# Deformable attention near the grid: both image rows of a half tile in one product, and a fourth predicated copy

## The chip, the cores and the metric

The kernel runs on one core of a Trainium2 chip. The metric is device time in microseconds (us) of one whole execution. Six runs of the kernel before lie between 7702.01 and 7724.52 us, with a median of 7711.0 us.

## What is computed

The program is a network of four layers over x of shape (4, 64, 64, 128): four images of 64 by 64 positions with 128 channels. Only the first layer's convolution part, a deformable attention, is touched. Its reference, cut to what matters:

```python
# q, k, v: 1x1 projection of x, then a depthwise 3x3; four groups of 32 channels
for i in range(4):
    off = conv1x1(pconv(q_img, ...), w_off[i], b_off[i])      # 9 taps x (dy, dx) per position
    dil = 2 * i + 1                                           # 1, 3, 5, 7
    k_i = deform_sample(k[i], off, mask, dil, dil)            # bilinear, at tap + offset
    v_i = deform_sample(v[i], off, mask, dil, dil)
attn = softmax(einsum('bgnc,bgckn->bgnk', q * 32 ** -0.5, ks))   # 9 taps
out = einsum('bgnk,bgckn->bgnc', attn, vs) @ w_proj + b_proj
```

A bilinear sample whose offset is under one position in size is a weighted sum over the 3 by 3 neighbours of its tap. So a query's logit at a tap is a weighted sum of its products with the 9 keys around the tap. The kernel tests the offsets once and takes this local path (`deformable_near`) when they are all that small, as they are here.

## The kernel before, in words

`deformable_near` (from line 609) goes through 128 tiles. Tile T is a pair of image rows, 128 positions; tiles 32b to 32b+31 are image b. A tile has two halves of 32 columns (h), and each half two image rows (r). The partition of a position is 64h + 32r + 8m + x: m is a block of 8 columns, x the place in it. Four neighbouring tiles form a chunk c.

**Queries (lines 712 to 725).** `products` copies the queries of a tile with GpSimd into `qm`, which is zero but for the 8 queries of block m in the weights `qm[rows, j, m]`, 32 columns wide, j = 2h + r. Two such buffers alternate. The queries come from DRAM 16 image rows at a time (`rows_of_queries`, line 734, 512 KB each).

**Products (lines 739 to 757).** `product` multiplies queries with keys on TensorE in float32. For each block m of 8 columns, each j and each of the four dilations g (one per group of 32 channels, and so per group of 32 rows of the array), a matmul takes 32 by 32 weights from `qm` and streams 3 tap rows x 3 key rows x CW[g] key columns past them, CW = 12, 16, 20, 24: 108, 144, 180 or 216 columns. It writes 32 partitions of the PSUM tile S of its dilation and sums over m. That is 64 matmuls a tile. In the trace each stands as two weight loads (PEld) and two matmul records (PE).

**Copies (line 759).** `copy_products` moves the four S tiles to SBUF (`band`, with room for the four tiles of a chunk) on ScalarE, four copies a tile. There is one buffer of each S, so the next product waits for them; `band` has two.

**Attention (lines 765 to 793).** Once a chunk, on VectorE. A query at x in its block has its neighbours x columns further right, so three predicated copies (shift 4, 2 and 1, chosen by the bits of the partition's number, in `bit`) bring the rows of `band` into line, for each dilation: 12 copies a chunk (line 772). Twelve multiplications with the bilinear weights H (line 774), a sum and the maximum follow. ScalarE takes the exponential (line 797), `spread` turns the weights into a banded matrix A (line 804 onward), `write` sends A to DRAM (line 825), and `read_dense` reads it back as dense rows D (line 836).

**Values.** Fourteen tiles after its product (LAG), a tile's D is transposed on TensorE (`transpose`, line 867, 12 instructions, copied to SBUF by ScalarE on line 869) and multiplied with values (`weigh`, line 887, up to 48 matmuls). Every fourth tile there is a projection (line 910).

**Order.** The text of the loop gives the order on TensorE: transpose of T-14, product of T, now and then a projection, weigh of T-14. `block` and `behind` hold TensorE to that. Elsewhere a scheduler sets the order on each engine, from the order of the text and from what each instruction waits for. As built, on ScalarE the exponential of chunk c stands ahead of the copies of tile 4c+5, and on GpSimd the multiplications that make H of chunk c+3 stand behind the query copies of tile 4c+6. So VectorE's attention of a chunk has to be over before the second tile after it can leave PSUM.

Of the kernel before, what the change touches and what calls it, by code (L numbers as in the profile page):

```python
# [10 lines left out]
F32 = mybir.dt.float32  # L11
I32 = mybir.dt.int32
# [348 lines left out]
def window(ap, off, dims):  # L361

    return bass.AP(ap.tensor, ap.offset + off, [list(ap.ap[0])] + dims)
# [245 lines left out]
def deformable_near(k, dr, x, y, qd, kd, vd, od, masks, w_proj, b_proj):  # L609
# [15 lines left out]

    nc, tc = k.nc, k.tc
    DIL = (1, 3, 5, 7)  # L630
    W = [2 * d + 3 for d in DIL]
    WB = [5, 9, 15, 21]
    CW = [w + 7 for w in W]
    PP = [12 * (15 + w) for w in W]
    with ExitStack() as ctx:
        wp = ctx.enter_context(tc.tile_pool(name="dn_w", bufs=1))
        sm = ctx.enter_context(tc.tile_pool(name="dn_s", bufs=2))
        ps = ctx.enter_context(tc.tile_pool(name="dn_ps", bufs=1, space=PSUM))
# [5 lines left out]
        bit = wp.tile([128, 1, 3], I32, tag="bit", name="bit")  # L644
        nc.sync.dma_start(bit[:, 0, :], masks)
        kpad = wp.tile([128, 80, 80], F32, tag="kpad", name="kpad")
        nc.gpsimd.memset(kpad, 0.0)

        qms = [wp.tile([128, 4, 4, 32], F32, tag=f"qm{i}", name=f"qm{i}") for i in range(2)]
        for t in qms:  # L650
            nc.gpsimd.memset(t, 0.0)

# [18 lines left out]
        Hs, bands, outs, vblocks, logits, ofs, hat_of, queries = {}, {}, {}, {}, {}, {}, {}, {}  # L671
        accs, lefts, project, stores = {}, {}, [], []
# [6 lines left out]
        def block(do, *args):  # L679

            with behind():
                last[0] = do(*args)
# [31 lines left out]
        def products(T):  # L714
            i = T % 32
            c, t = divmod(T, 4)
            if t == 0:
                bands[c] = [sm.tile([128, 3, 4, 3, CW[g]], F32, tag=f"band{g}", name=f"band{g}") for g in range(4)]
            qm = qms[T % 2]
            q = queries[T // 8]  # L720
            for h in range(2):
                nc.gpsimd.tensor_copy(
                    window(qm, 256 * h, [[128, 2], [40, 4], [1, 8]]),
                    q[:, 2 * (i % 8) : 2 * (i % 8) + 2, 32 * h : 32 * h + 32].rearrange("p y (m x) -> p y m x", m=4),
                )

        def rows_of_keys(n):
# [4 lines left out]
            )  # L732

        def rows_of_queries(n):
            b, h = divmod(n, 4)
            queries[n] = sm.tile([128, 16, 64], F32, tag="q", name="q")
            nc.sync.dma_start(queries[n], qd[b].rearrange("p (y x) -> p y x", x=64)[:, 16 * h : 16 * h + 16, :])

        def product(T, half):
            if half == 0:  # L740
                accs[T] = [ps.tile([128, 9, CW[g]], F32, tag=f"S{g}", name=f"S{g}") for g in range(4)]
            i, qm, acc = T % 32, qms[T % 2], accs[T]
            for m in range(2 * half, 2 * half + 2):
                for j in range(4):
                    h, r = divmod(j, 2)
                    for g, d in enumerate(DIL):
                        rows = slice(32 * g, 32 * g + 32)
                        v = kpad[rows]
                        keys = bass.AP(
                            v.tensor, v.offset + (8 + 2 * i + r - d - 1) * 80 + 8 + 32 * h + 8 * m - d - 1,  # L750
                            [list(v.ap[0]), [80 * d, 3], [80, 3], [1, CW[g]]],
                        )
                        ins = nc.tensor.matmul(  # L753
                            acc[g][32 * j : 32 * j + 32].rearrange("p (a s) c -> p a s c", a=3),
                            qm[rows, j, m, :], keys, start=(m == 0), stop=(m == 3),
                        )
            return ins

# [6 lines left out]
        def attention(c):  # L765
            H, band = Hs[c], bands.pop(c)
            prod = sm.tile([128, 4, 36, 9], F32, tag="prod", name="prod", bufs=1)
            for g in range(4):
                flat = band[g].rearrange("p a t s c -> p (a t s) c")
                for i, s in enumerate((4, 2, 1)):  # L770
                    n = W[g] + s - 1
                    nc.vector.copy_predicated(flat[:, :, 0:n], bit[:, :, i : i + 1].to_broadcast([128, 36, n]), flat[:, :, s : s + n])  # L772
                for tx in range(3):
                    nc.vector.tensor_tensor(
                        window(prod, 324 * g + 9 * tx, [[27, 12], [3, 3], [1, 3]]),
                        window(band[g], DIL[g] * tx, [[3 * CW[g], 12], [CW[g], 3], [1, 3]]),
                        window(H, 324 * g + 9 * tx, [[27, 12], [3, 3], [1, 3]]), op=ALU.mult,
                    )
# [12 lines left out]
            nc.vector.tensor_tensor(lg, lg, each, op=ALU.subtract)  # L791
            logits[c] = lg, m, me, taps, wide, each
# [137 lines left out]
        rows_of_queries(0)  # L930
        offsets(0)
        products(0)
        for T in range(128 + LAG):
            with behind():
                step(T, -1, products)
                step(T, -2, offsets, 4)
                step(T, 0, hats, 4)
                step(T, 1, lambda c: hat_products(c, (0, 1)), 4)
                step(T, 2, lambda c: hat_products(c, (2, 3)), 4)
                step(T, 4, attention, 4)  # L940
                step(T, 7, spread, 4)
                step(T, 9, write, 4)
                step(T, LAG - 2, read_dense)
                step(T, LAG, values)
            V, P = 0 <= T - LAG, T < 128
            late = list(stores)
            if V:
                block(transpose, T - LAG)
            if P:
                block(product, T, 0)  # L950
                block(product, T, 1)
            if project:
                block(projection, *project.pop())
            if V:
                block(weigh, T - LAG)
            with behind():
                if late:
                    store()
                step(T, 0, copy_products)
                step(T, LAG, values_done)  # L960
                if T % 8 == 4 and T < 124:
                    rows_of_queries(T // 8 + 1)
                if T < 96:
# [9 lines left out]
def prep_conv0(w):  # L973
    g = lambda n: w["L0_conv_" + n]
    off = lambda a: a.reshape(4, 9, 2, -1).transpose(2, 0, 1, 3).reshape(72, -1)
    p = np.arange(128)
    grid = np.zeros((128, 2, 4, 3, 3), np.float32)
    for i in range(4):
        step = (np.arange(3) - 1) * (2 * i + 1)
        grid[:, 0, i] = (p // 64)[:, None, None] + step[None, :, None]  # L980
        grid[:, 1, i] = (p % 64)[:, None, None] + step[None, None, :]
    return {
        "c0_w_qkv": g("w_qkv"), "c0_b_qkv": g("b_qkv").reshape(3, 128).T, "c0_w_dw": g("w_dw").reshape(3, 128, 9).transpose(1, 0, 2),
        "c0_b_dw": g("b_dw").reshape(3, 128).T,
        "c0_pconv": np.concatenate([g("pconv_off_w"), g("pconv_mask_w")[None]]).reshape(5, 32, 32, 9).transpose(1, 0, 3, 2),
        "c0_w_offT": np.concatenate([off(g("w_off")), g("w_mask")]).T,
        "c0_b_off": np.concatenate([off(g("b_off"))[:, 0], g("b_mask")]),
        "c0_grid": grid.reshape(128, 72),
        "c0_masks": np.stack([p // 4 % 2, p // 2 % 2, p % 2], axis=1).astype(np.int32), "c0_w_proj": g("w_proj"), "c0_b_proj": g("b_proj"),
    }  # L990


# [1614 lines left out]
```

## Time and profile before

| what | us |
|---|---|
| median of six runs | 7711.0 |
| the profiled execution, whole | 7687.94 |
| its span, first to last instruction | 7686.1 |
| `deformable_near`: first product to last weigh | 678 to 1823 |
| tiles 0 to 13, products alone | 678 to 770 |
| tiles 14 to 127, products and values (114 steps) | 770 to 1750 |
| last 14 tiles, values alone | 1750 to 1823 |

| 770 to 1750 us | busy us of 980 | a step (of 8.60 us) |
|---|---|---|
| TensorE matmuls | 735.96 | 6.46 |
| VectorE | 492.79 | 4.32 |
| ScalarE | 321.44 | 2.82 |
| GpSimd | 398.29 | 3.49 |
| DMA, mean share of 16 engines | 0.71 | 6.1 |

How to read it: all steps of the middle stretch do the same work, so 980 us / 114 gives one step, and the busy time of an engine can be divided the same way. The profiled execution is 23 us shorter than the median of the runs. DMA is given as a mean share over 16 engines, 0.71 x 8.60 = 6.1 us of all sixteen a step. In the names, `PEld` is TensorE's weight load, `PE` its matmul; SP issues most of the DMAs, ScalarE the others.

### The profile page before, as it was taken

The page shows a single profiled execution, that of the slowest core. Times are in us where ns is not written, and L with a number is a line of the kernel's source. Part 1 is how long each engine was busy: PE and PEld are TensorE (multiplying, and loading weights), DVE is VectorE, ACT ScalarE, POOL GpSimd, SP SyncE. Part 2 cuts the span into 40 slices and gives each one's busy share as a digit, 9 for nine tenths or more (in the row PEclk, how much of TensorE's full clock was granted, in tenths as well). Part 3 has the DMA queues.
Part 4 walks back from the last instruction along what each step waited for, and adds up shares of the span by engine and source line. Part 5 has one row for each costly group of instructions (what it writes and reads, how often), then busy time and mean ns, then how long its engine had stood idle before and what let it go on. Part 6 is the DMA issues. An engine that isn't in the chain of part 4 may idle for free. (4 is left out here: it accounts for less than half of the span.)

```text
span 7686.1 us, 173919 instructions
## 1 busy us (share of the span) xinstructions
PE 6524.1 (85%) x71983; PEld 3530.2 (46%) x71983; DVE 4663.4 (61%) x11050; ACT 2679.8 (35%) x6141; POOL 1753.1 (23%) x1634
## 2 busy tenths in 40 slices
PE   7996777775688868979989999798798997997989
PEld 3343656563456544345555555445225224242244
DVE  2214555454277654858855666675785885867877
ACT  3331333333234323611145656565104013031056
POOL 0003443430001100035532222154012012120135
PEclk9997888987788889989988999798897997998989
DMA  4436677775400022031000000001111111111101
GB/s 120 100 89 183 191 212 204 205 202 167 143 4 1 2 60 48 4 119 27 23 16 9 10 9 8 9 1 30 38 25 41 34 31 43 25 35 38 25 23 31
DMA packets 676539, 496.62 MB, mean 65 GB/s; under 512 B 302070, under 2 KB 593848, under 8 KB 671896
## 3 DMA queue, kind: packets, MB, share of 16 engines
q1 hardware_dynamic: 478606, 354.58, 17.0%
q10 hardware_dynamic: 197130, 130.77, 6.2%
q8 instruction: 572, 9.37, 0.5%
q14 instruction: 231, 1.89, 0.1%
HBM read 335.28 MB, written 149.75 MB: 63 GB/s over the span
## 5 line engine op out<-in xcount | busy, mean ns | idle before, releaser
L2476 DVE TENSOR_TENSOR t<-S,q 128x1536 f32<-128x1536 f32 (+3 forms) x608 | 1157.0, 1948 | 121.2 <-PE S L2464 115.9
L2464 PE MATMUL S<-R,L 32*128 32x512 f32 x4096 | 734.5, 651 | 89.9 <-DMA R<-wd 78.5
L2492 PE MATMUL acc<-t,sum 128*32 128x512 f32 x4096 | 639.6, 608 | 0.0
L772 DVE COPY_PREDICATED band<-bit,band 128x288 f32<-128x288 int32 (+11 forms) x384 | 244.1, 748 | 468.5 <-ACT band L763 450.7
L753 PE MATMUL S<-kpad,qm 32*32 32x216 f32 (+3 forms) x16384 | 398.0, 344 | 138.8 <-issue 78.4
L2178 PE MATMUL pe<-ew,yT 128*128 128x512 f32 x1024 | 479.3, 602 | 26.3 <-DVE xs L2184 23.3
L1777 PE MATMUL acc<-w,attT 128*64 128x264 f32 x4096 | 485.7, 390 | 11.9 <-DVE w L1773 11.9
L2464 PEld LDWEIGHTS S<-R,L 32*128 32x128 f32 x4096 | 200.3, 186 | 611.0 <-issue 279.9
L2498 ACT COPY agg<-acc 128x512 f32<-128x512 f32 x32 | 18.7, 585 | 1191.8 <-DMA L<-pd 681.4
L1770 POOL TENSOR_TENSOR w<-xtl,ei 128x528 f32<-128x528 f32 x256 | 331.8, 1317 | 314.1 <-ACT ei L1769 204.4
L2184 DVE SCALAR_TENSOR_TENSOR xs<-pe,gate,xs 128x128 f32<-128x128 f32 x1024 | 332.8, 345 | 96.2 <-PE pe L2178 79.6
L753 PEld LDWEIGHTS S<-kpad,qm 32*32 32x32 f32 x16384 | 275.9, 110 | 230.5 <-issue 133.3
L1773 DVE TENSOR_TENSOR w<-xtl,pe 128x1056 f32<-128x1056 f32 x256 | 320.2, 1251 | 101.4 <-ACT ei L1769 88.8
L1777 PEld LDWEIGHTS acc<-w,attT 128*64 128x64 f32 x4096 | 283.7, 137 | 198.6 <-DVE w L1774 38.3
L2187 ACT ACTIVATE sc<-pe,gate 128x128 f32<-128x128 f32 x1024 | 290.3, 374 | 200.8 <-PE pe L2178 193.7
L2507 POOL TENSOR_TENSOR o<-o,bf 128x512 f32<-128x512 f32 x32 | 40.6, 1269 | 1228.1 <-ACT o L2506 1228.1
L514 PE MATMUL dw<-pad,diag 32*32 32x512 f32 x6912 | 308.0, 617 | 11.2 <-ACT dwo L522 5.8
L887 PE MATMUL out<-dt,vb 128*32 128x32 f32 x12000 | 177.7, 208 | 149.4 <-issue 141.2
L2492 PEld LDWEIGHTS acc<-t,sum 128*32 128x32 f32 x4096 | 92.7, 108 | 458.6 <-issue 436.2
L763 ACT COPY band<-S 128x108 f32<-128x108 f32 (+3 forms) x512 | 113.7, 308 | 514.1 <-PE S L753 175.6
L2178 PEld LDWEIGHTS pe<-ew,yT 128*128 128x128 f32 x1024 | 185.4, 193 | 232.7 <-issue 151.0
L869 ACT COPY dt<-pt 128x512 f32<-128x512 f32 x384 | 209.4, 598 | 208.2 <-PE pt L867 201.6
(519 smaller groups left out, 12911.1 us busy)
## 6 DMA issues: line engine op xcount, KB each, us to landing
vb<-vd SPq DMA_DIRECT2D x272, 256.0 KB
D<-dd ACTq DMA_DIRECT2D x128, 192.0 KB
D<-dd SPq DMA_DIRECT2D x128, 168.0 KB
D<-dd ACTq DMA_DIRECT2D x128, 144.0 KB
w<-in_e_weight_dram ACTq DMA_DIRECT2D x16, 1024.0 KB
w<-in_e_weight_dram SPq DMA_DIRECT2D x16, 1024.0 KB
wd<-s SPq DMA_DIRECT2D x32, 512.0 KB
D<-dd SPq DMA_DIRECT2D x128, 120.0 KB
```

Source lines behind the costliest of these rows:

```text
L514: nc.tensor.matmul(acc[g][32 * c : 32 * c + 32], diag[r, j, tap, :], pads[j][r, y0 : y0 + 8, tx : tx + 64], start=(tap == 0), stop=(tap == 8),
L753: ins = nc.tensor.matmul(acc[g][32 * j : 32 * j + 32].rearrange("p (a s) c -> p a s c", a=3), qm[rows, j, m, :], keys, start=(m == 0), sto ...
L772: nc.vector.copy_predicated(flat[:, :, 0:n], bit[:, :, i : i + 1].to_broadcast([128, 36, n]), flat[:, :, s : s + n])
L1770: nc.gpsimd.tensor_tensor(w2[:, 2:4], xt[:, 2:4, 0:2], window(ei, 0, [[0, 2], [0, 2], [1, 132]]), op=ALU.mult)
L1773: nc.vector.tensor_tensor(w1, xt[:, :, 1:3], window(pe, 0, [[0, 4], [0, 2], [1, 132]]), op=ALU.mult)
L1777: nc.tensor.matmul(acc[b // 2][64 * (b % 2) : 64 * (b % 2) + 64], attT[:, b // 2, hp, 64 * (b % 2) : 64 * (b % 2) + 64], src[:, b].rearran ...
L2178: nc.tensor.matmul(pe[h].rearrange("p e c -> p (e c)"), yT[:, 128 * t : 128 * t + 128], ew[:, 4 * h : 4 * h + 4, :].rearrange("p e c -> p ...
L2184: nc.vector.scalar_tensor_tensor(xt, pe[0][:, e, :], gate[:, t, e : e + 1], xt, op0=ALU.mult, op1=ALU.add)
L2187: nc.scalar.activation(sc[:, e, j, :], pe[1][:, e, :], AF.Copy, scale=gate[:, t, 4 + e : 5 + e])
L2464: nc.tensor.matmul(S[:, j, :], Ls[n % 2][r, ag, :], Rs[n % 2][r, ag].rearrange("p x y -> p (x y)"), start=True, stop=True)
L2476: nc.vector.tensor_tensor(t[:, j0:j1].rearrange("p u (x y) -> p u x y", x=8), S[:, j0:j1].rearrange("p u (x y) -> p u x y", x=8), qf[:, q0 ...
L2492: nc.tensor.matmul(acc[0][32 * h : 32 * h + 32, :], sum4, t[:, j, :], start=(u < 4), stop=(u >= 60))
```

## The change

One matmul now serves both image rows of a half tile. Its weights are 64 columns wide (both rows' 8 queries of block m, at 32r + 8m), it streams 4 key rows instead of 3 (144, 192, 240 or 288 columns), and it writes 64 partitions of S. So there are 32 matmuls a tile instead of 64. Row r = 0 needs key rows 0 to 2 and row r = 1 key rows 1 to 3. S and `band` hold 4 key rows, and a fourth predicated copy for each dilation moves key rows 1 to 3 down by one on the partitions with r = 1: 12 runs of 3 CW elements. The other three copies work on the same sizes as before, in rows that now lie 4 CW apart. The queries come 8 image rows at a time (32 loads of 256 KB instead of 16 of 512 KB).

```diff
-        qms = [wp.tile([128, 4, 4, 32], F32, tag=f"qm{i}", name=f"qm{i}") for i in range(2)]
+        qms = [wp.tile([128, 2, 4, 64], F32, tag=f"qm{i}", name=f"qm{i}") for i in range(2)]
...
-                    window(qm, 256 * h, [[128, 2], [40, 4], [1, 8]]),
+                    window(qm, 256 * h, [[32, 2], [72, 4], [1, 8]]),
...
-            for m in range(2 * half, 2 * half + 2):
-                for j in range(4):
-                    h, r = divmod(j, 2)
+            for m in range(4):
+                for h in range(2):
                     for g, d in enumerate(DIL):
...
-                            v.tensor, v.offset + (8 + 2 * i + r - d - 1) * 80 + 8 + 32 * h + 8 * m - d - 1,
-                            [list(v.ap[0]), [80 * d, 3], [80, 3], [1, CW[g]]],
+                            v.tensor, v.offset + (8 + 2 * i - d - 1) * 80 + 8 + 32 * h + 8 * m - d - 1,
+                            [list(v.ap[0]), [80 * d, 3], [80, 4], [1, CW[g]]],
...
-                            acc[g][32 * j : 32 * j + 32].rearrange("p (a s) c -> p a s c", a=3),
-                            qm[rows, j, m, :], keys, start=(m == 0), stop=(m == 3),
+                            acc[g][64 * h : 64 * h + 64].rearrange("p (a s) c -> p a s c", a=3),
+                            qm[rows, h, m, :], keys, start=(m == 0), stop=(m == 3),
...
-                flat = band[g].rearrange("p a t s c -> p (a t s) c")
+                rows = lambda off, dims: window(band[g], off, [[4 * CW[g], 12]] + dims)
+                n = 3 * CW[g]
+                nc.vector.copy_predicated(rows(0, [[1, n]]), bit[:, 0, :, 3:4].to_broadcast([128, 12, n]), rows(CW[g], [[1, n]]))
                 for i, s in enumerate((4, 2, 1)):
                     n = W[g] + s - 1
-                    nc.vector.copy_predicated(flat[:, :, 0:n], bit[:, :, i : i + 1].to_broadcast([128, 36, n]), flat[:, :, s : s + n])
+                    nc.vector.copy_predicated(
+                        rows(0, [[CW[g], 3], [1, n]]), bit[:, :, :, i : i + 1].to_broadcast([128, 12, 3, n]), rows(s, [[CW[g], 3], [1, n]])
+                    )
...
-                if T % 8 == 4 and T < 124:
-                    rows_of_queries(T // 8 + 1)
+                if T % 4 == 1 and T < 124:
+                    rows_of_queries(T // 4 + 1)
```

More of the change, by code (lines that the diff above doesn't have):

```diff
@@ L643, in deformable_near @@
         nc.sync.dma_start(bpj[:, 0, :], b_proj.partition_broadcast(128))
-        bit = wp.tile([128, 1, 3], I32, tag="bit", name="bit")
-        nc.sync.dma_start(bit[:, 0, :], masks)
+        bit = wp.tile([128, 1, 1, 4], I32, tag="bit", name="bit")
+        nc.sync.dma_start(bit[:, 0, 0, :], masks)
         kpad = wp.tile([128, 80, 80], F32, tag="kpad", name="kpad")
         nc.gpsimd.memset(kpad, 0.0)
-        qms = [wp.tile([128, 4, 4, 32], F32, tag=f"qm{i}", name=f"qm{i}") for i in range(2)]
+        qms = [wp.tile([128, 2, 4, 64], F32, tag=f"qm{i}", name=f"qm{i}") for i in range(2)]
         for t in qms:
@@ L717, in products @@
             if t == 0:
-                bands[c] = [sm.tile([128, 3, 4, 3, CW[g]], F32, tag=f"band{g}", name=f"band{g}") for g in range(4)]
+                bands[c] = [sm.tile([128, 3, 4, 4, CW[g]], F32, tag=f"band{g}", name=f"band{g}") for g in range(4)]
             qm = qms[T % 2]
-            q = queries[T // 8]
+            q = queries[T // 4]
             for h in range(2):
                 nc.gpsimd.tensor_copy(
-                    window(qm, 256 * h, [[128, 2], [40, 4], [1, 8]]),
-                    q[:, 2 * (i % 8) : 2 * (i % 8) + 2, 32 * h : 32 * h + 32].rearrange("p y (m x) -> p y m x", m=4),
+                    window(qm, 256 * h, [[32, 2], [72, 4], [1, 8]]),
+                    q[:, 2 * (i % 4) : 2 * (i % 4) + 2, 32 * h : 32 * h + 32].rearrange("p y (m x) -> p y m x", m=4),
                 )
@@ L734, in rows_of_queries, with product @@
         def rows_of_queries(n):
[L735 to L741, printed above, removed]
+            b, h = divmod(n, 8)
+            queries[n] = sm.tile([128, 8, 64], F32, tag="q", name="q")
+            nc.sync.dma_start(queries[n], qd[b].rearrange("p (y x) -> p y x", x=64)[:, 8 * h : 8 * h + 8, :])
+        def product(T):
+            accs[T] = [ps.tile([128, 12, CW[g]], F32, tag=f"S{g}", name=f"S{g}") for g in range(4)]
             i, qm, acc = T % 32, qms[T % 2], accs[T]
-            for m in range(2 * half, 2 * half + 2):
-                for j in range(4):
-                    h, r = divmod(j, 2)
+            for m in range(4):
+                for h in range(2):
                     for g, d in enumerate(DIL):
@@ L775, in attention @@
                         window(prod, 324 * g + 9 * tx, [[27, 12], [3, 3], [1, 3]]),
-                        window(band[g], DIL[g] * tx, [[3 * CW[g], 12], [CW[g], 3], [1, 3]]),
+                        window(band[g], DIL[g] * tx, [[4 * CW[g], 12], [CW[g], 3], [1, 3]]),
                         window(H, 324 * g + 9 * tx, [[27, 12], [3, 3], [1, 3]]), op=ALU.mult,
@@ L949, in deformable_near @@
             if P:
-                block(product, T, 0)
-                block(product, T, 1)
+                block(product, T)
             if project:
@@ L988, in prep_conv0 @@
         "c0_grid": grid.reshape(128, 72),
-        "c0_masks": np.stack([p // 4 % 2, p // 2 % 2, p % 2], axis=1).astype(np.int32), "c0_w_proj": g("w_proj"), "c0_b_proj": g("b_proj"),
+        "c0_masks": np.stack([p // 4 % 2, p // 2 % 2, p % 2, p // 32 % 2], axis=1).astype(np.int32), "c0_w_proj": g("w_proj"), "c0_b_proj": g("b_proj"),
     }
```

## The prediction

> **What bounds the kernel now.** I read the windows first, then who waits, the DMA queues, the timeline and the groups. The window of the 114 steps that do both products and values (columns: length, busy time and instructions by engine, granted clock, DMA share, GB/s):
>
> ```profile
> 770.00:1750.00 980.00, 735.96 (x26677) 595.21 (x26664) 492.79 (x1503) 321.44 (x878) 398.29 (x544) 0.88 0.71 202
> ```
>
> TensorE (first pair) is busy 75% of it, and nothing else is busier. The waits of TensorE in the same stretch say what fills the other 244 us:
>
> ```profile
> PE out L887 <- issue: 134.8, 78, 4.3
> PE S L753 <- issue: 76.0, 66, 3.5
> PE pt L867 <- issue: 11.8, 6, 3.2
> PE S L753 <- POOL qm L722: 6.3, 8, 1.3
> PE pr L910 <- issue: 5.8, 2, 3.6
> PE S L753 <- ACT band L763: 3.9, 3, 3.1
> ```
>
> Four rows end in "issue", 228 us together: no semaphore is waited for, the engine has nothing to issue. The DMA queues of the stretch and TensorE's timeline tell why:
>
> ```profile
> q8 instruction: 209, 3.42, 1.5%
> ```
>
> ```profile
> 1205.84 0.40 PE L887 MATMUL out<-dt,vb 128*32 128x32 f32 x24 [0.89 <-issue]
> 1206.17 1.64 PE L867 MATMUL pt<-ident,D 128*128 128x128 f32 x12
> 1207.74 1.83 PE L753 MATMUL S<-kpad,qm 32*32 32x108 f32 x91
> 1211.42 1.08 PE L753 MATMUL S<-kpad,qm 32*32 32x144 f32 x37 [1.85 <-issue]
> ```
>
> Queue q8 brought 209 packets of 16 KB; 26677 + 26664 matmuls and weight loads over 209 packets are 255 each. Between the two stalls stand 24 + 12 + 91 matmuls, with their weight loads some 255 again. So TensorE runs dry at packet ends. In the trace, packets start 4.70 us apart in the mean (a twentieth under 3.5, a twentieth over 6.8); 186 of 209 are followed, 1.4 us after they land, by the end of a stall. **TensorE is bound by the arrival of its instructions:** busy 735.96 / 209 = 3.52 us a packet, waiting 1.1.
>
> **The change part by part, for one step of 8.60 us.**
>
> *Fewer instructions.* 53341 / 114 = 468 matmuls and weight loads a step. A product has 64 matmuls x 4 records = 256; it gets 128. So 340 remain, 1.33 packets for 1.83. At 4.70 us a packet that is 6.25 us.
>
> *The streams.* The groups by form:
>
> ```profile
> L753 PE MATMUL S<-kpad,qm 32*32 32x216 f32 x4096 | 384.6, 397 | 19.1 <-issue 18.7
> ...
> L753 PE MATMUL S<-kpad,qm 32*32 32x108 f32 x4096 | 332.2, 288 | 79.9 <-POOL qm L722 39.2 <-issue 21.0 <-ACT band L763 19.1
> ...
> L2367 PE MATMUL po<-pn 32*64 32x64 f32 x2048 | 87.2, 337 | 0.0
> ```
>
> 397 - 288 ns over 108 columns is 1.01 ns a column, and 179 ns that don't depend on it. One position of the array is visited by 4 blocks x 2 records in turn: 8 x 216 x 1.01 = 1.75 us for dilation 7, + 0.18 = 1.9 us, where a product is busy 2.99 us (341.1 us of the stretch / 114). With 288 columns the same chain is 2.3 + 0.18 = 2.5 us, the lower end; with the old excess of 1.06 us kept, 3.6, the upper. Half as many weights should shrink the excess: I take 2.9, no gain. The form 32*64 stands on line 2367: 243.2 us busy for 6144 records, 40 ns each at 337 ns long, so such tiles overlap. TensorE is then busy 6.46 - 2.99 + 2.9 = 6.4 us a step, 4.8 a packet.
>
> *The two together.* A packet now takes as long to work off (4.8) as the next one to come (4.7, spread about 1.05): the wait does not vanish, about half the packets are late. With a spread of 0.7 for the work, the mean lateness is 0.4 x sqrt(1.05² + 0.7²) = 0.5 us; 1.33 x 0.5 = 0.7, and 6.4 + 0.7 = **7.1 us a step**, 1.5 less. 114 x 1.5 = 171 us.
>
> The Trainium skill, "Runtime: NRT & Kernel Launch", section "Instruction fetch mechanics", agrees on blocks of 256 instructions but calls the cost of crossing one mostly hidden. By it the instruction count is worth nothing and the change brings about 0.1 us a step, 10 in all; the rows above speak against it. "TensorEngine Tiling (Array Packing)", section "Available Configurations", has 16 tiles of 32x32 but 8 of 32x64: by that count alone a product would take 4/3, 4.0 us, and a step 8.0 or so. The busy time of 2.99 against a chain of 1.9 says that the tiles were not what bound it.
>
> *The fourth predicated copy,* 4 more a chunk. An old one of a dilation takes 475 to 1000 ns and hardly depends on its shift: its mean is near 1.1 ns x 36 x CW. The new ones have as many elements, 12 x 3 CW, 2592 together: by these rows 475 + 650 + 820 + 990 = 2.9 us. By the reduction on line 781 (1503 ns for 1296 elements) 3.0; by the dearest row (482 ns for 180) 2.7 x 2592 = 6.9, the upper end. I take 3.0, the shape being nearest to whole rows; the old ones overlap (244.1 us busy for 384 of 748 ns: 0.85), so 2.6. VectorE goes from 4.32 to 5.0 us a step: hidden in its idle time:
>
> ```profile
> DVE band L772 <- ACT band L763: 415.2, 28, 19.9
> ```
>
> But it lengthens the path copies of tile 4c+3, attention, exponential, copies of 4c+5. Attention now lasts 11.9 us (1193.4 to 1205.3), then 14.5. Behind the exponential on ScalarE wait the copies of 4c+5, and for them the product of 4c+6. From their end to the copies of 4c+7 are two steps, less transpose and weigh, already done by then (230.0 + 155.7 us / 113 = 3.4): 14.2 - 3.4 = 10.8. The circle is 14.5 - 0.6 (overlap) + 0.35 + 0.9 + 10.8 = 26 us for four steps, under 28.4. Covered, by 2.4 us; without that cover each us more costs 0.25 a step.
>
> *Copies out of PSUM:* 248 to 372 ns for 108 to 216 elements, 1.15 ns each; 216 elements more a tile, 0.25 us, beside 3.4 us of transpose and weigh. Nothing.
>
> *Queries:* GpSimd copies as many elements; nothing. 16 more SP issues of 0.45 us, 7 us over 980 of a queue that issues 5.6 us a step (now of 7.1): nothing. They stand between dense reads four tiles ahead of use; late ones would hold GpSimd and then the product.
>
> *DMA:* the same bytes in less time, 6.1 / 7.1 = 86% busy. Instruction packets share the engines with them; in the trace, with 16 or more packets in flight the next instruction packet starts 2.5 us after a stall's end, with under 4 in flight 1.4. I leave the mean at 4.7; 5.2 would cost 0.4 us a step.
>
> *First 14 tiles:* in their window TensorE waits 33.0 us for qm from GpSimd, 15.1 for copies of S, and only 2.4 on issue; nothing gained, three attentions of 2.6 us more, at most 8: I take 6. *Last 14:* no products; the last attention has 50 us until its tiles come: nothing.
>
> Sum: -171 + 6 = -165 us. The profiled execution of 7688 becomes 7523; it ran 23 us under the median of 7711, from which I forecast **7546**.
>
> **The rivals.**
>
> *Fed, but not faster (a step of 7.5 to 8.0).* TensorE's chain takes the place of the wait: a product at its upper 3.6 makes 7.1 busy and about 7.7 a step, -97 us. Or VectorE's circle: attention at its upper end of 18.8 makes 30.3 / 4 = 7.6, -110 us. For: both lie within 0.6 us of the bound. Against: the 1.06 us excess looks like issue, and the copies' rows are even.
>
> *Better (6.5).* Refills stay at 4.7, the product falls to 2.5, the clock (0.88) rises because TensorE pauses less: -235 us. Against: DMA would be 94% busy.
>
> *It does nothing.* Refills slow down as DMA grows denser, a packet coming every 6.4 us: 1.33 x 6.4 = 8.5, no change. Against: even with 16 in flight the delay grew by 1.1 us only.
>
> *Slower.* The fourth copy in VectorE's circle: it decides once four steps exceed 34.4 us, that is attention above 22.6 + 0.3 us, the new copies over 11 us a chunk. At twice the dearest row, 5.4 ns x 2592 = 14 us, attention is 25.9, the circle 37.3, 9.3 us a step: +0.7 x 114 = +80 us. For: no row shows a copy of 12 long runs whose source overlaps its target. Against: no f32 row costs a third of that.
>
> **How the numbers follow.** Forecast (6.8 to 7.4 a step) 0.52; fed but not faster 0.19; better 0.17; nothing 0.05; slower 0.07. The predicted time is that of the first. From -240 to -60 us holds 8 in 10: 7470 to 7650. Within 0.2% (15 us, about what measurement can tell from no change) 0.05; faster 0.88; slower 0.07.
>
> **What would show it.** Right: some 152 packets on q8 in the middle stretch instead of 209, about 4.9 us apart; "issue" under 130 us instead of 228; a product busy near 2.9 us; the new copies 0.5 to 1 us each; ScalarE's wait for line 791 small. Wrong: packets 6 us apart; TensorE waiting for S copies behind the exponential; a product over 3.6 us.

## The result

The changed kernel takes 7691.8 us (median of 37 runs), the kernel before 7705.6 us (77 runs): the ratio is 0.9984, 95% interval 0.9978 to 0.9990, some 12 us less. The forecast was 7546. The two profiled executions lie closer still, 7686.57 against 7687.94.

By stages of the profiled executions (before, after): tiles 0 to 13 take 88.1 and 93.2 us, a step of tiles 14 to 127 takes 8.67 and 8.54 us (by the starts of the products), the last 14 tiles take 76.8 and 79.7. So the middle gained 113 x 0.13 = 15 us, where 171 had been forecast, and the ends lost 8.

The window of the middle stretch, in the columns of the one shown of before:

```profile
770.00:1750.00 980.00, 740.88 (x19763) 619.20 (x19752) 666.64 (x1654) 330.33 (x886) 371.22 (x541) 0.84 0.71 205
```

TensorE did its work with 74% of the instructions, and its busy time, like its idle time, is what it was: 239 us idle for 244. The DMA share did not move either, 0.71 and 205 GB/s for 202. What TensorE waits for is another matter (waited for, total us, times, longest):

```profile
PE S L750 <- ACT band L760: 103.1, 48, 6.1
PE S L750 <- POOL qm L721: 73.6, 14, 9.4
PE out L888 <- issue: 44.9, 34, 4.7
PE S L750 <- issue: 4.7, 3, 3.4
PE pt L868 <- issue: 4.7, 4, 2.4
```

The queue of instruction packets:

```profile
q8 instruction: 155, 2.54, 1.1%
```

155 packets for 209, and 54 us of "issue" for 228: the wait that the change was priced by is gone. In its place stand 103 us for ScalarE's copies of S, which free the PSUM that the next product writes, and 74 us for GpSimd's copies of queries. Both had been 10 us together. 174 us went and 167 came.

So why are those copies late? ScalarE's waits after the change:

```profile
ACT band L760 <- DMA D<-dd: 138.4, 27, 7.2
ACT lg L798 <- DMA D<-dd: 82.3, 10, 11.2
ACT band L760 <- DMA dd<-A: 50.1, 13, 5.2
ACT lg L798 <- DMA kpad<-kd: 49.7, 6, 9.6
```

and the same engine before:

```profile
ACT dt L869 <- PE pt L867: 172.2, 145, 5.5
ACT band L763 <- DMA D<-dd: 155.9, 35, 7.9
...
ACT band L763 <- DMA dd<-A: 22.0, 5, 5.0
```

A copy of S into `band` reads neither D nor dd. The releaser belongs to what stands ahead of the copy on ScalarE: half of the dense reads (line 837) are issued there. In the program as built, all transfers that SyncE and ScalarE issue share eight semaphores in turn (in the trace the numbers 100 and 102 to 108), and each waits at its issue for the landing of the one eight before it. That is a limit of the program and not of the chip: at most eight transfers in flight. There are 45 of them in four steps, and each lands 4.2 us after its issue has ended, 4.8 us after it began. One place shows how it reaches TensorE. SyncE's queue, ScalarE's and TensorE, in three views of the timeline of after (start, length, engine, instruction, how often in a row; in brackets the idle time before it):

```profile
1262.85 5.68 SPq L826 DMA_DIRECT2D dd<-A  x7
1268.63 1.27 SPq L837 DMA_DIRECT2D D<-dd  x2
```

```profile
1263.14 1.61 ACT L870 COPY dt<-pt 128x512 f32<-128x512 f32 x3
1269.20 1.22 ACTq L837 DMA_DIRECT2D D<-dd  x2
1270.46 1.07 ACT L760 COPY band<-S 128x144 f32<-128x144 f32 x4 [5.71 <-DMA D<-dd]
```

```profile
1263.51 2.20 PE L750 MATMUL S<-kpad,qm 32*64 32x144 f32 x64
1265.64 1.04 PE L888 MATMUL out<-dt,vb 128*32 128x32 f32 x96
1266.61 1.63 PE L868 MATMUL pt<-ident,D 128*128 128x128 f32 x12
1270.88 4.56 PE L750 MATMUL S<-kpad,qm 32*64 32x144 f32 x64 [2.64 <-ACT band L760]
```

The product ends at 1265.7 and ScalarE is idle, but it stands at its next dense read until 1269.20: the transfer eight before is one of SyncE's writes, which landed at 1269.18. The copies start 4.8 us late, TensorE 2.64 us late, and its next product runs at half the speed, 4.56 us for 2.20. Over tiles 20 to 123, such waits at ScalarE's issues (idle time over 0.15 us ahead of an issue whose own semaphore came last) add up to 223 of 907 us before and 379 of 893 us after; the expectations below have 205 and 358, by another count. For 347 of the 379 us the transfer eight before was in flight; for the rest SyncE had not issued it yet or was issuing it.

The same can be followed for all of TensorE's waits on ScalarE in the stretch. For 93 of the 103 us, ScalarE's last idle time ahead of the copy ended with the landing of a DMA, for 5 us with VectorE. In 50 of the 93 us it is the exponential that stood at the transfers, ahead of the copies.

GpSimd in the same stretch of after:

```profile
POOL xg L905 <- DMA xg<-in_x_dram: 350.8, 20, 24.8
```

The sum of tokens and bias stands ahead of the copies of queries, and waits for a load that comes late in the same line of transfers. With two smaller rows such waits are 456 us; before, they were 208.5 ("issue") and 44.8 us. For 71 of the 74 us that TensorE waits for queries, GpSimd's last idle time was of this kind.

### The profile page after: what moved, and what is told of

It is laid out like the page before. It is cut to its first block, busy times and chain, and to the rows that moved or that the text cites. A ratio compares the mean times of both kernels' runs of the same rounds, so it can differ in the third digit from the quotient of the medians.

```text
span 7683.6 us, 157708 instructions
## 1 busy us (share of the span) xinstructions
PE 6518.5 (85%) x63791; PEld 3548.7 (46%) x63791; DVE 4828.8 (63%) x11178; ACT 2687.1 (35%) x6141; POOL 1727.9 (22%) x1634
## 5 line engine op out<-in xcount | busy, mean ns | idle before, releaser
L750 PE MATMUL S<-kpad,qm 32*64 32x288 f32 (+3 forms) x8192 | 412.5, 425 | 236.9 <-POOL qm L721 119.7
L750 PEld LDWEIGHTS S<-kpad,qm 32*64 32x64 f32 x8192 | 306.5, 157 | 293.9 <-issue 138.4
L760 ACT COPY band<-S 128x144 f32<-128x144 f32 (+3 forms) x512 | 136.0, 351 | 458.6 <-DMA D<-dd 146.2
L768 DVE COPY_PREDICATED band<-bit,band 128x432 f32<-128x432 int32 (+3 forms) x128 | 108.5, 902 | 256.8 <-ACT band L760 216.6
L868 PE MATMUL pt<-ident,D 128*128 128x128 f32 x1536 | 236.7, 309 | 17.5 <-DMA D<-dd 8.2
```

The source lines that it names most:

```text
L750: ins = nc.tensor.matmul(acc[g][64 * h : 64 * h + 64].rearrange("p (a s) c -> p a s c", a=3), qm[rows, h, m, :], keys, start=(m == 0), sto ...
```

## The experiments

Times are ratios to the kernel before, run beside each kernel on the same chip; the change itself is 0.9984. Each expectation spells out the theories that it weighs.

**Without the fourth copy.** The changed kernel less the one new line on VectorE (so the lower image row's products stay out of line in the result).

```diff
-                nc.vector.copy_predicated(rows(0, [[1, n]]), bit[:, 0, :, 3:4].to_broadcast([128, 12, n]), rows(CW[g], [[1, n]]))
```

> The changed kernel without its four predicated copies a chunk that move key rows 1 to 3 down (left out: that move, so the products of every second image row stay out of line). Theory A, the circle of VectorE and ScalarE: in the changed kernel copies of tile 4c+3, attention (15.0 us), exponential (2.9 us later, behind two dense-read issues on ScalarE), copies of tile 4c+5, product of 4c+6 set the four steps of 34.5 us. Without the copies attention lasts 12.0 us and the scheduler puts the exponential ahead of the reads: four steps of 29 to 32 us, 70 to 150 us less than the kernel after. Theory B, transfers: ScalarE and GpSimd are held by landings of dense reads and of the token loads, and VectorE's length does not matter: within 15 us of the kernel after.

Measured: 0.9964 (0.9948 to 0.9981), some 15 us under the changed kernel, give or take 14. Attention is back at 12 us and VectorE at 495 us, and TensorE still waits for the same engines, most of all for ScalarE's copies of the transposed D:

```profile
PE out L887 <- ACT dt L869: 77.6, 32, 4.7
PE S L750 <- ACT band L760: 61.7, 30, 6.6
PE pt L867 <- ACT o L912: 35.1, 14, 5.7
PE S L750 <- POOL qm L721: 32.0, 24, 2.5
```

The fourth copy takes about a tenth of the missing gain of 153 us, at most a fifth. The edit also moved the exponential: here it stands ahead of the next dense reads on ScalarE, in the changed kernel behind two of them. So the 15 us are for both together, and VectorE's circle as the main cause falls.

**The kernel before, with copies of the same size added** (each onto itself, so the result stays).

```diff
+                wide = band[g].rearrange("p a t s c -> p (a t) (s c)")
+                nc.vector.copy_predicated(wide, bit[:, :, 3:4].to_broadcast([128, 12, n]), wide)
...
```

> The kernel before with four more predicated copies a chunk of the size of the new ones (12 runs of 3 CW elements, each onto itself). As built, the exponential stands behind two dense-read issues on ScalarE, as in the changed kernel. Theory of the prediction: 3 us more of VectorE a chunk are hidden while instructions bound TensorE: within 15 us of the kernel before. Theory A: attention and exponential push the copies of tile 4c+5 from 17.2 to 18 to 20 us after those of 4c+3: 20 to 70 us slower. Theory B: no change.

Measured: 1.0035 (1.0021 to 1.0050), 27 us more, in the range of theory A: the edit is not free even where instructions bind. It too put the exponential behind two dense reads, so the 27 us are not the copies' alone. ScalarE's waits at its issues rise from 223 to 416 us, and without the fourth copy they had fallen from 379 to 327. Why a longer attention brings them is not shown; it may move the bursts of writes against the reads.

**The copies of S first on ScalarE**, ahead of the exponential and the dense reads; in the changed kernel and in the kernel before.

```diff
-                step(T, LAG - 2, read_dense)
...
+                with tc.issue_after(copied[min(T, 127)].ins):
+                    step(T, LAG - 2, read_dense)
...
+            with tc.issue_after(copied[min(4 * c + 5, 127)].ins):
+                nc.scalar.activation(lg, lg, AF.Exp, scale=32 ** (-0.5))
```

> The changed kernel with one order set on ScalarE: each tile's four copies of S stand ahead of that step's dense-read issues, and the exponential of chunk c behind the copies of tile 4c+5. Theory A: those copies then end about 11.6 us after the ones of 4c+3 instead of 18.5, and the product of 4c+6 starts 4 to 5 us earlier: 100 to 200 us less than the kernel after, four steps of 28 to 31 us. Theory B: the reads are issued later and bind as before: no gain, or slower.

> The kernel before with the same order on ScalarE. If the arrival of instructions bounds TensorE there, as the prediction read it, this is worth little: 0 to 30 us less than the kernel before, with the waits on issue still near 228 us in the middle stretch. If the order on ScalarE was the bound of the kernel before as well, it gains as much as in the changed kernel, 100 us or more.

Measured: 1.0058 (1.0036 to 1.0080) and 1.0040 (1.0027 to 1.0052), both slower. Theory A misses; theory B, which expected no gain or a loss, holds. The waits moved on. The reads now come late themselves, and the changed kernel's transposes wait 88 us for them; its DMA share fell to 0.68. But the exponential came later as well, 7.9 us after its logits were ready for 2.5, and GpSimd's waits for VectorE behind it grew from 34 to 238 us. The run doesn't tell the two apart. In the kernel before, 0 to 30 us less had been expected at issue waits near 228 us; these fell to 156, and waits for D and for ScalarE took their place.

**All dense reads on SyncE**, in both kernels.

```diff
-                (nc.sync, nc.scalar)[g % 2].dma_start(
+                nc.sync.dma_start(
```

> The changed kernel with all dense reads issued by SP, none by ScalarE. The first runs put theory A aside (3 us less of VectorE brought 14 us). Theory C: in the program each of the 45 transfers of four steps waits, at its issue, for the landing of the one issued eight before it; the traces show 6.1 to 6.3 in flight, 4.2 us from issue to landing, and ScalarE standing 358 us of 893 in front of such issues (205 of 907 in the kernel before), with the copies out of PSUM behind them. With the reads on SP only transfers wait: TensorE's waits for copies and exponential go, 80 to 170 us less than the kernel after. If the eight in flight bound by their number alone, wherever they are issued (theory C strict): within 30 us of the kernel after. Theory B, bandwidth: the same.

> The kernel before with all dense reads issued by SP. The arrival of instructions, 4.7 us a packet, bounds TensorE at 34.3 us for four steps there: 0 to 25 us less than the kernel before, waits on issue still over 200 us in the middle stretch. If what held the kernel before was ScalarE in front of its transfers, it gains as much as the changed one, over 60 us.

Measured: 1.0049 (1.0033 to 1.0065) and 0.9999 (0.9984 to 1.0014). Before does not care, and its issue waits stay at 225 us: ScalarE's blocked queue was covered there by TensorE's wait for instructions. The changed kernel gets 50 us slower, where theory C expected 80 to 170 us less and its strict form no change: a miss for all. SyncE issues for 702 of 968 us, and TensorE waits longer for GpSimd:

```profile
PE S L750 <- POOL qm L721: 173.1, 33, 11.6
PE S L750 <- ACT band L760: 79.0, 22, 5.4
```

The second row is of another kind than in the changed kernel. ScalarE issues nothing here and never stands at a transfer; its exponential waits 175 us for VectorE's logits, and the copies of S stand behind it. That is the circle of the prediction, which binds as soon as the reads are out of ScalarE's way.

**The writes split in two** in the changed kernel: 16 more transfers in four steps, same bytes, same rows.

```diff
+                    for u in (0, 2):
...
+                            A[g][32 * j : 32 * j + 32, u : u + 2, 0 : W[g]].rearrange("p t c s a -> p t (c s a)"),
```

> The changed kernel with each of the 16 writes of A of a chunk split into two of half the size: 61 transfers in four steps instead of 45, the same bytes. Theory C, by number in flight: four steps grow from 34.4 to 40 to 47 us, 150 to 350 us slower than the kernel after. Theory B, bandwidth: within 30 us of it. A split write of half the size may land sooner, which takes from C's number and not from its sign.

Measured: 1.0245 (1.0228 to 1.0262), 200 us more, 10.17 us a step. TensorE's first wait and ScalarE's:

```profile
PE S L750 <- ACT band L760: 226.8, 67, 8.3
```

```profile
ACT band L760 <- DMA D<-dd: 351.9, 49, 10.4
```

Theory C's range holds. The bytes are the same and the DMA share fell to 0.60, so it isn't bandwidth: more transfers in the line cost, through ScalarE. Whether by the limit of eight is not shown. SyncE issues the 16 more one after another, 28.6 us of issuing in four steps for 22.1, and the step's growth is as large. In 308 of ScalarE's 621 us at its issues, the transfer eight before had not been issued yet or was being issued; in the changed kernel that was 33 of 379.

**Reads on SyncE, and the loads of tokens, offsets and queries on GpSimd's own queue**, which has semaphores of its own.

```diff
-                nc.sync.dma_start(xg, tokens(x, b, 4 * c, 4))
+                nc.gpsimd.dma_start(xg, tokens(x, b, 4 * c, 4))
...
```

> The changed kernel with the dense reads on SP and the loads of tokens, offsets and queries issued by GpSimd, whose transfers wait on semaphores of their own: 42 transfers in the ring of eight instead of 45. Theory C: 10 to 60 us less than with the reads on SP alone, less what GpSimd pays for issuing. Theory B: no gain.

Measured: 0.9993 (0.9980 to 1.0006). That is 43 us under the reads on SyncE alone, in theory C's range, and no gain over the changed kernel. ScalarE is out of the way, and GpSimd holds TensorE alone:

```profile
PE S L750 <- POOL qm L721: 242.4, 30, 16.2
...
PE S L750 <- ACT band L760: 1.0, 1, 1.0
```

GpSimd itself waits 300 us for the store of the tokens' buffer, still in SyncE's line, at the issue of the next load.

**One read a tile for four dilations**, in both kernels (the scratch laid out as one, 33 transfers in four steps); and with the bias added behind the projection's sum.

```diff
+            nc.sync.dma_start(
+                dense[t].rearrange("p g n -> p (g n)"),
+                bass.AP(m.tensor, m.offset + t * 1536, [[16 * 6156, 8], [6144, 16], [1, 1536]]),
...
```

> The changed kernel with its four scratch tensors of coefficients laid out as one, so that one transfer reads a tile's dense coefficients (all four dilations, 1536 values a row) where four did: some 33 hardware transfers per four steps for 45, at 147 KB a step more (about 8% more bytes); all on SyncE, none on ScalarE. Theory C (the number of transfers in flight, held at eight by the program's semaphores, took the gain): the ring no longer fills, TensorE's waits for ScalarE's copies shrink from 103 us to under 40, and the gain that the prediction had named appears: a step of 7.2 to 8.0 us, 7540 to 7640 us. Rival D (the DMA engines' bytes, busy 71%): 8% more bytes make it no faster, 7690 to 7780. Rival E (GpSimd's queue alone holds the step, whatever the transfers do): waits for qm stay at 70 to 170 us, 7680 to 7700.

> The kernel before with the same merged reads. Theory C: before is bound by the arrival of its instructions, the ring had slack: TensorE's issue waits stay over 190 us and the time within 0.4%, 7675 to 7720. Rival D: more bytes, 7720 to 7800. If the number of transfers bound the kernel before as well, it gains as much as the changed one, 7550 to 7640.

> As the one with merged reads, and GpSimd adds the bias to the tokens behind the projection's sum and not ahead of it, so that its wait for the tokens' load no longer stands ahead of the copies of queries. Theory C: the load comes in time anyhow with a free ring, so it is within 20 us of the merged reads alone. Theory E: TensorE's waits for qm fall to under 20 us, and it is 40 to 120 us faster than the merged reads alone.

Measured: 1.0527 (1.0502 to 1.0553), 1.0480 (1.0451 to 1.0509) and 1.0514 (1.0484 to 1.0544): a miss for every theory. The rival of bytes had the sign, and far too small a size; only the late bias came as theory C had it, within 20 us of the merged reads alone. The issue view has a read of 768 KB, and the packets of 6 KB took 435 ns each, where those of 1.5 KB had taken 78; those of 2 KB rose from 105 to 134. The window of the changed kernel:

```profile
770.00:1740.00 970.00, 564.91 (x14176) 467.44 (x14180) 456.73 (x1192) 251.17 (x643) 276.17 (x402) 0.72 0.69 159
```

159 GB/s at a DMA share of 0.69, so this edit made each byte dearer. It doesn't test the number of transfers.

**Only the late bias.**

```diff
-                nc.gpsimd.tensor_tensor(xg, xg, bpj.to_broadcast([128, 4, 128]), op=ALU.add)
...
             nc.gpsimd.tensor_tensor(xg, xg, o, op=ALU.add)
+            nc.gpsimd.tensor_tensor(xg, xg, bpj.to_broadcast([128, 4, 128]), op=ALU.add)
```

> The changed kernel with only the late bias on GpSimd (the reads stay four a tile, on SyncE and ScalarE). Theory C: the waits for qm (74 us) go, but the ring stays full and ScalarE's copies come late instead: a step of 8.4 to 8.6 us, 7670 to 7700. Theory E: 7600 to 7650.

Measured: 0.9988 (0.9974 to 1.0002), no change, as the line of transfers would have it:

```profile
PE S L750 <- ACT band L760: 144.0, 58, 7.3
...
PE S L750 <- POOL qm L721: 2.0, 2, 1.1
```

Theory E misses. 72 us of waits for GpSimd went and 41 us came at ScalarE; the steps of the middle got to 8.36 us and the first 14 tiles lost 4 us of it. GpSimd's queue is not the cause; it is one of two doors.

**Without half of the writes**, in both kernels (8 fewer transfers in four steps, 5% fewer bytes).

```diff
-            for g in (1, 2, 3, 0):
+            for g in (2, 3):
```

> The changed kernel without the writes of the coefficients of dilations 1 and 3 to the scratch (so these dilations' values are left out of the result): 8 of 45 transfers fewer in four steps, but only 336 KB of some 7000 KB, 5% of the bytes. Theory C (transfers in flight): 16 more cost 6.8 us in four steps, so 8 fewer bring some 3 us: a step of 7.7 to 7.9 us, 7590 to 7640 us. Rival D (bytes): at most 5% of the DMA's time, and the DMA is busy 71% only: 7660 to 7690. Rival E (GpSimd's or VectorE's queue): no change, 7680 to 7700.

> The kernel before with the same writes left out (so the values of dilations 1 and 3 are left out of the result). Theory C: before is bound by the arrival of its instructions, so freer transfers bring little: 7660 to 7700, issue waits over 190 us in the middle stretch. If transfers bound the kernel before just as much, it gains what the changed one gains, 7590 to 7640.

Measured: 0.9920 (0.9895 to 0.9945) and 0.9971 (0.9956 to 0.9987). The changed kernel gains 49 us and before some 22, at issue waits of 236 us. The changed kernel comes in just above theory C's range, and its step of 8.2 us (in the profile of the slowest of four runs) misses C's 7.7 to 7.9. ScalarE's waits at its issues fall to 234 us, but TensorE now waits 127 us for GpSimd, 108 of them while GpSimd waits for the load of offsets. The gap between the two kernels grows from 0.16% to 0.5% (0.2 to 0.8, by the intervals), in the direction that the line of transfers asks for.

**Reads merged by pairs** (37 transfers, 4% more bytes, rows of 2.6 and 3.0 KB), and that with the late bias.

```diff
+            for kk, x0 in enumerate((72, 792)):
+                m, P = dd[c % 2][kk], PR[kk]
+                (nc.sync, nc.scalar)[kk].dma_start(
+                    flat[:, x0 : x0 + P],
...
```

> The changed kernel with the reads of dense coefficients merged by pairs of dilations (two a tile instead of four, one on SyncE and one on ScalarE): 37 transfers in four steps for 45, 4% more bytes, rows of 2.6 and 3.0 KB. Theory C: a step of 7.7 to 8.2 us, 7590 to 7650 us. Rival D: 4% more bytes and longer packets, 7690 to 7800. Rival E: 7680 to 7700.

> As the reads merged by pairs, with GpSimd's bias behind the projection's sum as well. Theory C: ScalarE and GpSimd both free of the ring, 7570 to 7650 us, within 30 us of the pair reads alone. Rival D: as the pair reads alone, 7690 to 7800. Rival E: 40 us or more faster than the pair reads alone.

Measured: 1.0082 (1.0058 to 1.0107) and 1.0072 (1.0045 to 1.0099). Slower, as rival D, the bytes, had it, so the number alone is not it either: fewer transfers took 5.3 us each to land for 4.2, 5.9 of them in flight on the mean.

**Half of each dense read left out**, in both kernels: 45 transfers as ever, a fifth of the bytes gone.

```diff
-                    dense[t][:, g, 12 * (7 - d) : 12 * (7 - d) + P],
+                    dense[t][:, g, 12 * (7 - d) : 12 * (7 - d) + P // 2],
```

> The changed kernel with each read of dense coefficients cut to the first half of its row (the other half stays zero, so part of the weights is left out of the result): still 45 transfers in four steps, but 1.25 MB of some 7.05 MB fewer, 18%. Theory D (the DMA engines are as full at 71% busy as eight transfers in flight let them be, and that held the step at 8.5 us): the transfers' floor falls from 34.4 to some 29 us in four steps, TensorE's own work and packets bind again: 7.1 to 7.7 us a step, 7530 to 7610 us. Theory C in its first form (the number of transfers alone): 7670 to 7700. Rival E (the queues of GpSimd and VectorE): no better than with the writes left out, 7630 to 7660, with over 100 us of waits for qm.

> The kernel before with the same reads cut to half. Theory D: it is bound by the arrival of its instructions as well as by the transfers, so with these lighter 20 to 50 us go and no more: 7655 to 7690, issue waits over 190 us in the middle stretch; the changed kernel with the same cut is then 70 to 140 us faster than this one. If the instructions' packets come sooner on emptier DMA engines, 7590 to 7650, and the issue waits fall under 170 us.

Measured: 0.9890 (0.9858 to 0.9921) and 0.9877 (0.9845 to 0.9908). Both gain 70 to 95 us, and they are level: the forecast lead of 70 to 140 us for the changed one did not appear, and its step of 7.87 us misses theory D's 7.1 to 7.7. TensorE's waits, changed and then before:

```profile
PE S L750 <- ACT band L760: 107.9, 47, 6.2
PE S L750 <- POOL qm L721: 38.6, 14, 7.5
PE out L888 <- issue: 32.8, 39, 2.0
```

```profile
PE out L887 <- issue: 133.5, 84, 3.1
PE S L753 <- issue: 55.3, 61, 3.0
```

Before still waits for instructions, but its packets come 4.35 us apart instead of 4.70: 1.83 packets x 4.35 = 7.97 us, and a step is 7.98. Its time lies in the range given for instructions that come sooner, though its issue waits, 200 us, are not under the 170 that went with it. So lighter data transfers bring instructions sooner, and the kernel before gets its share. The changed kernel, at 7.87 us a step, still waits for ScalarE, which stands at its issues for 339 of 823 us (before with the same cut: 62 of 834), 73 times of 134 behind one of SyncE's writes.

The runs side by side (transfers and times per four steps of the middle; bytes are the window's GB/s times that time; in flight is counted from the start of an issue to its landing):

| kernel | transfers | MB | GB/s | in flight | four steps, us |
|---|---|---|---|---|---|
| before | 44.5 | 7.0 | 202 | 6.1 | 34.7 |
| after | 44.8 | 7.0 | 205 | 6.3 | 34.2 |
| after, writes split | 60.8 | 6.9 | 170 | 5.8 | 40.7 |
| after, pair reads | 36.8 | 7.2 | 200 | 5.9 | 36.2 |
| after, fewer writes | 36.7 | 6.6 | 201 | 5.8 | 32.8 |
| after, half reads | 44.8 | 5.6 | 179 | 5.2 | 31.5 |
| before, half reads | 44.5 | 5.7 | 178 | 5.2 | 31.9 |

No kernel had more than 6.8 transfers in flight on the mean, or a DMA share in these stretches over 0.73.

## Why the prediction was wrong, step by step

*Fewer instructions:* right. 155 packets where 152 were named, issue waits of 54 us where under 130 were. The packets came 6.3 us apart, which the prediction names as a sign of being wrong; but as TensorE's waits on issue fell, late packets aren't what held it. That TensorE was bound by the arrival of its instructions before agrees with the reads put on SyncE, which left that kernel's time alone. The Trainium skill, "Runtime: NRT & Kernel Launch", section "Instruction fetch mechanics", calls crossing a block mostly hidden; here the waits fell by 174 us with the packets, so by measurement it was not hidden. That the time hardly fell does not speak for that page: something else filled the gap.

*The streams:* right in sum, by luck. TensorE is busy 740.88 / 114.7 = 6.46 us a step, 6.4 had been worked out. But a product takes 2.20 us in half of the cases without a stall ahead of it, under the 2.5 that the prediction had as its lower end. Behind a stall of 0.15 to 2 us it mostly takes 2.88, and behind one of more than 2 us, 37 times of 114, it takes 2.9 to 4.8, mostly over 4. The mean of 3.15 (357.0 us for 7251 / 64 products; 2.9 forecast) holds the price of waits that the prediction did not foresee. The granted clock fell from 0.88 to 0.84.

*The fourth copy:* nearly right. The group of the new copies:

```profile
L768 DVE COPY_PREDICATED band<-bit,band 128x432 f32<-128x432 int32 (+3 forms) x128 | 108.5, 902 | 256.8 <-ACT band L760 216.6 <-DMA vb<-vd 34.0 <-issue 6.2
```

108.5 us over 32 chunks is 3.4 us a chunk, 3.0 had been taken; attention went from 12.0 to 15.0 us, 14.5 forecast. "Covered, by 2.4 us" was too kind. It let the exponential start at once; behind two dense reads on ScalarE it started 2.5 us after its logits were ready. With that and 15.0 us of attention the prediction's circle comes to 29 us, over its 28.4 but far under the 34.2 measured. The runs put copies and place of the exponential at some 15 us (left out of the changed kernel) and 27 (added to before). VectorE rose to 5.8 us a step and not 5.0, since the spreading of weights slowed down as well.

*First and last 14 tiles:* +5 where +6 was taken, and +3 where nothing was.

***DMA* and *copies out of PSUM*: this failed.** The prediction said "the same bytes in less time, 6.1 / 7.1 = 86% busy", and "Nothing" for the copies on ScalarE. It read the share of 0.71 as room to 1, and the copies as an engine with time to spare. No run's middle stretch got beyond 0.73: with eight transfers in flight at most, 0.71 seems close to what this program can get out of its queues, though no run tested that limit. And ScalarE's room was not free: 223 us before already went into waiting at its issues for earlier transfers, with the copies of S behind. The row `ACT band L763 <- DMA D<-dd: 155.9` stood in the profile of before and was not used. It cost nothing then, as the run of before with its reads on SyncE shows; with 174 us of TensorE's waits on issue gone, 103 us of waits for ScalarE's copies and 74 us for GpSimd's queries stood in their place. "TensorE waiting for S copies behind the exponential" was one of the prediction's own signs of being wrong, and 50 of the 103 us are of that kind. The rival "it does nothing" named the DMA too, but by slower instruction packets. That is not what happened, as TensorE's issue waits fell.

What is shown: the predicted wait went; waits for ScalarE and GpSimd took its place; in the changed kernel both engines stand at transfers, or at data that come late from them (93 of the 103 us and 71 of the 74); taking one out of the way makes the other late (late bias, loads on GpSimd), or VectorE's circle (reads on SyncE); more transfers at the same bytes slow it down strongly, and fewer bytes speed it up. What is not settled: how much the change is worth with the transfers wholly out of its way. With a fifth of the bytes gone it was worth nothing, with half of the writes gone 0.5%. Nor why the same queues collide more in the changed kernel (379 us against 223): the longer attention, or the place of the exponential that came with it, has a part in it (416 with the copies added to before, 327 without them after). That the exponential stands behind two dense reads isn't all of it: without the fourth copy it stood ahead of them, at 327 of 888 us and nearly the same time. Nor is the limit of eight told apart from SyncE's time for issuing. A version with more semaphores, or with the writes spread out in time, wasn't tried. None of the versions that compute the whole was faster than the changed kernel by more than the intervals.

## What to carry to other kernels

Before a wait is priced at its full length, read every in-order engine behind it for waits on a DMA whose data it does not use: that is a queue blocked at an issue, and it can become the bound as soon as the first one goes. A mean DMA share is no measure of room; count the transfers in flight and how long each takes to land against how many the program allows. And where instructions and data come by the same engines, lighter data transfers can help a kernel that is short of instructions as much as one that is short of data: here 95 and 72 us.

## What the runs showed of the hardware

Larger transfers were not better ones. The Trainium skill, "DMA: Bandwidth & Descriptors", section "Measured (HBM→SBUF, 128 partitions, SWDGE, issued from GpSimd)", advises to batch transfers to 1 MiB and more, from transfers issued by GpSimd. Here, issued by SyncE, reads of 768 KB in rows of 6 KB, 24,576 bytes apart, brought the whole from 205 to 159 GB/s, 435 ns a packet for 78; rows of 2592 and 2976 bytes took 129 and 173 ns, 50 and 58 ns a KB after 51. Whether the length of the row or the distance did it was not separated.

VectorE's small operations of the spreading slowed down in the changed kernel where nothing in them had changed: the multiplication into A from 379 to 443 ns, the copies of 24 elements from 279 to 507, and without the fourth copy they were at 365 and 242 again. The Trainium skill, "SBUF — State Buffer", section "SBUF: two separate sides", has VectorE and GpSimd exclude each other on a shared port. The traces fit that: the copies of 24 elements that ran while GpSimd was at work took 531 ns in the mean, the others 177, and 81 of 87 fell beside GpSimd's work in the changed kernel but 26 of 87 before (516 and 179 ns). The multiplications beside GpSimd's work took 582 ns, the others 357, 100 of 261 against 24 of 255. That the port is the reason, no run here shows.
